# Preparing the state's coefficients two chunks ahead, instead of one, across the end of the loop

## The chip, the cores and the metric

The kernel runs on one core of one Trainium2 chip. The metric is the device time of one execution in microseconds (us). Before the change the median of three runs is 31318.25 us (31296.25 to 31333.38).

## The reference, cut to what matters

Three layers work on 8 images of 128 channels and 64 x 64 pixels: a deformable convolution (nine taps, sampled at computed offsets), a state-space scan over the 4096 pixels of each image, and a mixture of experts. The scan sets the order of everything, as each step needs the state of the step before:

```python
x_proj = x @ W_in
xs, z = jnp.split(x_proj, 2, axis=-1)
delta = xs @ W_delta
Bv = xs @ W_B
Cv = xs @ W_C
deltaA = jnp.exp(jnp.einsum('bld,dn->bldn', delta, A))
deltaB = jnp.einsum('bld,bln->bldn', delta, Bv)
def step(state, inp):
    dA_i, dB_i, x_i, C_i = inp
    state = dA_i * state + dB_i * x_i[:, None, :]
    y = jnp.einsum('bdn,bn->bd', state, C_i)
    return (state, y)
```

The state has 256 x 256 elements for each of the 8 images. `deltaA`, the coefficient of the state, is as large, and it is new at every step.

## The kernel before, in words

First `prepare` and `images` lay out the weights, normalize the images, and write the table of pixels and the records of offsets to DRAM. Then 4096 steps of the scan run for all 8 images at once. A **block** is 16 steps (`BL`), a **chunk** two steps (`CH`), so a block has 8 chunks. The loop `For_i` (L1445) makes 8 passes; the body of a pass holds 32 blocks (`BODY`), that is 512 steps and 256 chunks (`NC`), written out. Between two passes all engines meet at a barrier that belongs to L1445.

What one chunk c needs before its steps can run:

- `load_rows` (L1129): 7 DMAs on SP's queue bring the rows of delta into `rt[c % 2]`. They wait until the decays of chunk c - 2, which read that buffer, are through.
- `decays` (L1179): 19 groups of matmuls (40 in all) on PE put the products of delta and A into PSUM banks. There are three banks for this and for all other matrix work.
- `grow` (L1208): ACT takes the exponential of each group (20 instructions) into `et[c % 2]` and so frees the bank. It waits until all products of chunk c - 2, which read the same buffer, are made.
- `load_terms` (L1142): 4 DMAs on SP's queue bring the factors of the added term into `uu[c % 2]`, after the last matmul of chunk c - 2 that reads it.
- `copy_c` (L1161): ACT copies C into `zc[c % 2]`, after the contractions of chunk c - 2.

`rt`, `uu`, `zc` and `et` have two buffers each.

What one step does: the state lies in five parts. POOL multiplies the coefficients with three of them, `ht`, in SBUF (`pair`, L1305, the products `mt`, `mt`, `m`), DVE with the two others, which accumulate in PSUM (`ud` and one half of the tile `yp`; products `md` and `mh`, copied back by ACT, L1333). PE makes the added terms from `uu` (`units`, L1274), DVE adds them to `ht` (L1328), and PE contracts the products with C into y (`contract`, L1351), which is the other half of `yp`, in two operations per step.

Beside the steps runs, per block, the work of other layers: `conv_load`, `conv_gather` (nine gathers per block on POOL, L727), `conv_scale`, `conv_mix` for a block ahead; `project` (the projections of a block ahead) and `stores` (to DRAM, from where `load_rows` and `load_terms` read). `behind` (L995) is the output chain of a block that is done: it waits for y, adds the skip term (L1003), multiplies with the gate (L1008), clears y (L1011), transposes (L1016), copies to `yt` (L1023), multiplies with W_out, adds the residual (L1031), normalizes, routes, runs the experts and stores the result (L1069). In the last block of a pass the whole of `behind` lies after the last step.

The order of the instructions on each engine is set by a planner in the kernel, `Schedule` (L120), at the time the program is written. Each piece of work is a generator that yields operations with a duration; the planner keeps a clock for each engine, takes the engine that could start first, and among the operations that could start on it within a short window (200 ns on PE, 100 on ACT and DVE, 50 on POOL) the one that is due first. Due times are in steps and come from `DUE` (L71): for chunk c the decays are due from 2(c - 1) - 0.1 over 1.61 steps, the exponentials from 2(c - 1) + 0.77 over 1.65; the contractions of step j at j + 1.65 and half a step later; the operations of `behind` for block b from 16(b + 1) + 0.16 over 13.12 steps, divided by 80. A due time is a priority, no delay: what is ready and finds its engine free is done.

The chunks that are ready when the loop begins are prepared by the same generators ahead of it (L1430 to L1443). What the body then prepares is shifted against what it consumes: at the end of a pass it prepares the first chunks of the next. `before` (L1384) lists the events that the planner may take as past when a pass begins. The ranges in these three places are what the change touches.

Of the kernel before, what the change touches and what calls it, by code (L numbers as in the profile page):

```python
# [31 lines left out]
NCH = BL // CH  # L32
# [24 lines left out]
NC = SPAN // CH  # L57
# [164 lines left out]
def kernel(  # L222
# [352 lines left out]
    rt = several(2, [KR, RROW], BF, "rt")  # L575
# [550 lines left out]
    def at_chunk(c):  # L1126
        return (c // NCH) % 2, c % NCH

    def load_rows(chunks):  # L1129
        for c in chunks:  # L1130
            k, i = at_chunk(c)
            yield Due(CH * c - 3)
            yield Wait(("rows_there", c // NCH), ("decayed", c - 2))
            for n in range(GD // 2):
                yield Op(
                    SP, 400, lambda c=c, k=k, i=i, n=n: nc.sync.dma_start(  # L1136
                        out=rt[c % 2][18 * n : 18 * n + 18, RW * n : RW * n + RW],
                        in_=cells(k, RW * i + 2 * RQ * n, ((NCH * RW, 18), (1, RW))),
                    ), lat=3500, sets=[("rt", c)] * (n == GD // 2 - 1), chain=False,
                )  # L1140

    def load_terms(chunks):  # L1142
        for c in chunks:
            k, i = at_chunk(c)
            yield Due(CH * c - 1)
            yield Wait(
                ("delta_there", c // NCH), ("b_there", c // NCH), ("summed", c - 2)
            )
            for p in range(QI // 2):
                yield Op(  # L1150
                    SP, 400, lambda c=c, k=k, i=i, p=p: nc.sync.dma_start(
                        out=uu[c % 2][32 * p : 32 * p + 9].rearrange(
                            "r w b l n -> r (w b) (l n)"
                        ),
                        in_=pr[k].rearrange("i j p w b l n -> p (i j) (w b) (l n)")[
                            p, :, :, CH * DIN * i : CH * DIN * i + CH * DIN
                        ],
                    ), lat=3500, sets=[("uu", c)] * (p == 3), chain=False,
                )

    def copy_c(chunks):  # L1161
        for c in chunks:
            k, i = at_chunk(c)
            yield Due(CH * c - 0.5)
            yield Wait(("ctt", c // NCH), ("contracted", c - 2))
            yield Op(
                ACT, 110, lambda c=c, k=k, i=i: nc.scalar.copy(
                    zc[c % 2].rearrange("p s x -> p (s x)")[
                        :, 31 : 31 + 32 * NH * QI * CH
                    ].rearrange("p (s x) -> p s x", x=32)[:, :, 0].rearrange(  # L1170
                        "p (m l) -> p m l", l=CH
                    ),
                    ctt[k].rearrange("p h (b c l) -> p (h b) c l", b=QI, l=CH)[:, :, i, :],
                ), sets=[("zc", c)], chain=False,
            )
# [3 lines left out]
    def decays(chunks):  # L1179
        for c in chunks:  # L1180
            rv = rt[c % 2].rearrange("p (q g t) -> p q g t", q=GD, t=CT)
            at, span = DUE["decay"]
            yield Due(CH * (c - 1) + at, span / NG)
            yield Wait(("rt", c), *early(c))
            for g in range(NG):
                fs, n = (1, GD) if g < NG - 1 else (2, P - NA * GD)
                m = n * CT

                def decay(ps, c=c, g=g, rv=rv, fs=fs, n=n, m=m):
                    held[c, g] = ps  # L1190
                    for h in range(NH):
                        for f in range(fs):
                            mm(
                                ps[:, m * (NH * f + h) : m * (NH * f + h + 1)].rearrange(
                                    "p (q t) -> p q t", q=n
                                ),
                                alhs[:KR, g + f, P * h : P * h + P], rv[:, :n, g + f, :],
                            )

                yield Op(  # L1200
                    PE, 198 if fs == 1 else 240, decay, need="bank", chain=False,
                    sets=[("dec", c, g)] + [("decayed", c)] * (g == NG - 1),
                )
# [4 lines left out]
    def grow(chunks):  # L1208
        for c in chunks:
            yield Wait(*[  # L1210
                ("prod", CH * (c - 2) + lo, p) for lo in range(CH) for p in range(5)
            ])
            ec = et[c % 2].rearrange("p l b h d -> p h (l b) d")
            at, span = DUE["exp"]
            yield Due(CH * (c - 1) + at, span / NG)
            for g in range(NG):
                yield Wait(("dec", c, g))
                ps = held.pop((c, g))
                if g < NG - 1:
                    fs, n, d0 = 1, GD, P * (g % 2) + GD * (g // 2)  # L1220
                else:
                    fs, n, d0 = 2, P - NA * GD, NA * GD
                m = n * CT

                def exps(ec=ec, ps=ps, fs=fs, n=n, d0=d0, m=m):
                    for f in range(fs):
                        nc.scalar.activation(  # L1227
                            ec[:, :, :, P * f + d0 : P * f + d0 + n],
                            ps[:, m * f * NH : m * (f + 1) * NH].rearrange(
                                "p (h d t) -> p h t d", h=NH, d=n  # L1230
                            ),
                            AF.Exp,
                        )

                yield Op(
                    ACT, 428 if fs == 1 else 210, exps, lat=165, free=[("bank", ps)],
                    sets=[("et", c)] * (g == NG - 1), chain=False,
                )
# [145 lines left out]
    def before(n):  # L1384

        keys = []
        for b in range(n - 4, n + 1):
            keys += [(w, b) for w in (
                "rows_there", "delta_there", "b_there", "projected", "ctt", "seen",
            )]  # L1390
        for b in range(n - 6, n):
            keys += [("seen_y", b), ("out", b), ("y", b)]
        for b in range(n - 4, n + 2):
            keys += [("scaled", b), ("mixed", b), ("tnt", b)]
        for c in range(NCH * (n - 3), NCH * n + 1):
            keys += [("rt", c), ("uu", c), ("zc", c), ("et", c)]
        keys.append(("rt", NCH * n + 1))
        keys.append(("pace", n + 2))
        keys += [("pace", n + 2, i) for i in range(TAPS) if turn_of(n + 2, i) < 0]
        for c in range(NCH * (n - 3), NCH * n):  # L1400
            keys += [("decayed", c), ("summed", c), ("contracted", c)]
            keys += [("prod", CH * c + lo, p) for lo in range(CH) for p in range(5)]
        keys.append(("decayed", NCH * n))
        return keys

    def start(events):
# [23 lines left out]
    with tc.manual_schedule():  # L1430
        s = start(past)
        s.add(conv_load(range(2), lambda b: BL * b))
        s.add(conv_gather(range(2)))
        s.add(conv_scale(range(2)))
        s.add(conv_mix(range(2)))
        s.add(project(range(1)))
        s.add(stores(range(1)))
        s.add(load_rows(range(2)))
        s.add(load_terms(range(1)))
        s.add(copy_c(range(1)))  # L1440
        s.add(decays(range(1)))
        s.add(grow(range(1)))
        s.run()  # L1443

    with tc.For_i(0, NBLOCK * BL, SPAN) as i0:  # L1445
        with tc.manual_schedule():
            s = start(before(0))

            def place(b):
                return i0 + BL * b  # L1450

            s.add(behind(range(BODY), place))
            for p in (3, 4, 0, 1, 2):
                s.add(pair(p, range(SPAN)))
            s.add(units(range(SPAN)))
            s.add(contract(range(SPAN)))
            s.add(decays(range(1, NC + 1)))
            s.add(grow(range(1, NC + 1)))
            s.add(load_rows(range(2, NC + 2)))
            s.add(load_terms(range(1, NC + 1)))  # L1460
            s.add(copy_c(range(1, NC + 1)))
            s.add(stores(range(1, BODY + 1)))
            s.add(project(range(1, BODY + 1)))
            s.add(conv_load(range(2, BODY + 2), place))
            s.add(conv_gather(range(2, BODY + 2)))
            s.add(conv_scale(range(2, BODY + 2)))
            s.add(conv_mix(range(2, BODY + 2)))
            s.run()
# [43 lines left out]
```

## Time and profile before

| | |
|---|---|
| runs, median (lowest to highest) | 31318.25 us (31296.25 to 31333.38) |
| profiled execution, time | 31319.12 us |
| its span, first to last instruction | 31317.4 us |
| mean granted TensorE clock | 0.975 |
| POOL products on 128 x 1024, 8192 of them | 2369 ns each |
| POOL products on 128 x 768, 4096 of them | 1825 ns each |
| gathers (L727), 2322 of them | 975 ns each |
| exponentials (L1227), 40980 of them | 527 ns each |
| first and last pass begin (first product on POOL) | 696.46 us, 27490.84 us |

A row of the profile names line, engine, operation, the tile written and the tiles read, the shapes, the count, then the busy time in us, the mean of one in ns, and the idle time of the engine just before, with what ended it. In the timeline a row is start (us), duration (us), engine, line, operation, tiles, shapes and count, and in brackets the idle time before it and its releaser. Almost all matmuls are recorded by a helper at L690, so that the tiles tell which they are: `bank<-rt,alhs` is a decay, `up<-uu` and `ud<-uu` an added term, `yp<-mt,zc` a contraction.

### The profile page before, as it was taken

What the parts mean: (1) busy time and instruction counts of PE and PEld (TensorE: products, weight loads), DVE (VectorE), ACT (ScalarE), POOL (GpSimd) and SP (SyncE); (2) the same over time, 40 slices, a digit from 0 to 9 for tenths busy, and PEclk for the clock granted to TensorE, in tenths of its full rate; (3) what the DMA queues carried; (4) which work ended last, traced back from release to release, by engine and by line L of the source; (5) the groups of instructions that cost most, each with busy time, mean ns of one, the idle gap of its engine ahead of it and who ended that gap; (6) DMA issues with size and microseconds to landing.
All of it is one profiled execution on the core that took longest, in us unless ns stands there. A gap on an engine that the chain in (4) does not pass through costs nothing. (4 is left out here: it accounts for less than half of the span.)

```text
span 31317.4 us, 832803 instructions
## 1 busy us (share of the span) xinstructions
PE 28316.2 (90%) x304277; PEld 15352.6 (49%) x304277; DVE 26365.3 (84%) x47787; ACT 25477.9 (81%) x57905; POOL 28804.5 (92%) x14692
## 2 busy tenths in 40 slices
PE   6999989999899998999989999899998999989998
PEld 3444544454444444444444444444544444444544
DVE  5888888888888888888888888888888888888888
ACT  2888888888888888888878888888888888878888
POOL 1999999999999999999999999999999999999999
PEclk7999999999999999999999999999999999999999
DMA  7222222222222222222222222222222222222222
GB/s 165 59 58 59 59 56 59 58 60 57 58 57 60 58 59 56 60 59 58 60 55 59 57 60 58 57 58 59 59 57 58 57 60 58 59 56 60 59 57 56
DMA packets 4785814, 1907.20 MB, mean 61 GB/s; under 512 B 3445459, under 2 KB 4595944, under 8 KB 4780656
## 3 DMA queue, kind: packets, MB, share of 16 engines
q1 hardware_dynamic: 4578504, 1187.48, 19.6%
q0 software_dynamic: 195232, 639.15, 7.5%
q8 instruction: 2421, 39.67, 0.6%
q10 hardware_dynamic: 7944, 26.87, 0.3%
q14 instruction: 1713, 14.03, 0.2%
HBM read 1284.96 MB, written 566.60 MB: 59 GB/s over the span
## 5 line engine op out<-in xcount | busy, mean ns | idle before, releaser
L1227 ACT ACTIVATE et<-bank 128x448 f32<-128x448 f32 (+1 forms) x40980 | 19046.1, 527 | 3611.4 <-PE bank L690 2990.6
L1313 POOL TENSOR_TENSOR mt<-et,ht 128x1024 f32<-128x1024 f32 x8192 | 19277.1, 2369 | 1450.0 <-PE yp L690 859.0
L690 PE MATMUL bank<-rt,alhs 126*128 126x224 bf16 (+1 forms) x81960 | 12265.7, 254 | 1450.1 <-ACT et L1227 648.7
L1328 DVE TENSOR_TENSOR ht<-mt,up 128x1024 f32<-128x1024 f32 x8192 | 9969.5, 1217 | 2637.0 <-PE ud L690 1846.6
L690 PEld LDWEIGHTS <-alhs 126*128 126x128 bf16 x81960 | 6761.8, 98 | 7657.1 <-issue 6817.9
L690 PE MATMUL yp<-mt,zc 128*32 128x256 f32 x65536 | 8711.5, 388 | 154.5 <-ACT yp L1333 57.0
L1313 POOL TENSOR_TENSOR m<-et,ht 128x768 f32<-128x768 f32 x4096 | 7476.9, 1825 | 38.2 <-DVE ht L1328 10.9
L690 PE MATMUL up<-uu 32*128 32x256 bf16 x45056 | 4832.3, 275 | 600.7 <-DVE ht L1328 521.6
L1313 DVE TENSOR_TENSOR md<-et,ud 128x1024 f32<-128x1024 f32 x4096 | 4975.0, 1215 | 113.3 <-PEq L1445 43.4
L690 PE MATMUL yp<-m,zc 128*32 128x256 f32 x24576 | 4449.4, 391 | 151.3 <-POOL m L1313 143.1
L1328 DVE TENSOR_TENSOR ht<-m,up 128x768 f32<-128x768 f32 x4096 | 3893.4, 951 | 566.3 <-PE up L690 524.6
L1333 ACT COPY ud<-md 128x1024 f32<-128x1024 f32 x4096 | 4275.3, 1044 | 97.4 <-DVE md L1313 84.9
L690 PE MATMUL yp<-md,zc 128*32 128x256 f32 x32768 | 4353.8, 387 | 0.0
L690 PEld LDWEIGHTS yp<-mt,zc 128*32 128x32 f32 x65536 | 3271.6, 109 | 1620.2 <-issue 533.9
L690 PEld LDWEIGHTS <-uu 32*128 32x128 bf16 x65541 | 1616.1, 92 | 3121.3 <-issue 2878.9
L727 POOL DMA_INDIRECT g<-table,rec x2322 | 2264.1, 975 | 413.9 <-issue 254.1
L690 PE MATMUL yp<-mh,zc 128*32 128x256 f32 x8192 | 2480.0, 385 | 0.0
L1313 DVE TENSOR_TENSOR mh<-et,yp 128x256 f32<-128x256 f32 x4096 | 1706.5, 417 | 446.0 <-PE yp L690 423.4
L690 PEld LDWEIGHTS yp<-m,zc 128*32 128x32 f32 x24576 | 1587.7, 109 | 921.5 <-issue 421.2
L1333 ACT COPY yp<-mh 128x256 f32<-128x256 f32 x4096 | 1596.2, 390 | 346.6 <-PE yp L690 207.4
L760 DVE SCALAR_TENSOR_TENSOR bank<-g,rec,bank 128x128 f32<-128x128 f32 x4644 | 1641.6, 353 | 84.6
L690 PE MATMUL ud<-uu 32*128 32x256 bf16 x16388 | 1621.5, 276 | 0.0
(207 smaller groups left out, 22799.8 us busy)
## 6 DMA issues: line engine op xcount, KB each, us to landing
rt<-rz SPq DMA_DIRECT2D x14350, 22.5 KB
uu<-pr SPq DMA_DIRECT2D x8196, 36.0 KB
pr<-dpt SPq DMA_DIRECT2D x3084, 48.0 KB
pr<-bpt SPq DMA_DIRECT2D x3084, 48.0 KB
rz<-dst SPq DMA_DIRECT2D x6939, 21.0 KB
table<-xc SPq DMA_DIRECT2D x24, 1690.0 KB
g<-table,rec POOLq DMA_INDIRECT x2322, 3.5
rec<-recs SPq DMA_DIRECT2D x2064, 2.8 KB
```

Source lines behind the costliest of these rows:

```text
L690: nc.tensor.matmul(out, lhs, rhs, start=start, stop=stop, **kw)
L727: nc.gpsimd.indirect_dma_start(out=g, out_offset=None, in_=table, in_offset=bass.IndirectOffsetOnAxis(ap=rec[b % 2].bitcast(I32)[:, j : j ...
L760: nc.vector.scalar_tensor_tensor(out, gq, s, acc, ALU.mult, ALU.add)
L1227: nc.scalar.activation(ec[:, :, :, P * f + d0 : P * f + d0 + n], ps[:, m * f * NH : m * (f + 1) * NH].rearrange("p (h d t) -> p h t d", h= ...
L1313: (nc.gpsimd if g < QP else nc.vector).tensor_tensor(like(g, m), part(g, c, lo), like(g, state[g]), ALU.mult)
L1328: lambda m=m: nc.vector.tensor_tensor(ht[g], m, up[:, :n], ALU.add),
L1333: ACT, act_ns(n, True), lambda m=m: nc.scalar.copy(state[g], m),
```

## The change

Everything that belongs to chunk 1 of a pass moves across the end of the loop: ahead of the loop the loads, decays, exponentials and the copy of C are made for chunks 0 and 1 instead of chunk 0 (and the rows of delta loaded for three chunks instead of two); the body prepares chunks 2 to 257 instead of 1 to 256 (rows: 3 to 258 instead of 2 to 257), and the events taken as past are extended accordingly. Buffers, due times and the operations themselves stay as they are. The pass thus ends with the decays and exponentials of chunk 257, which is chunk 1 of the next pass.

```diff
@@ -1392,15 +1392,15 @@
-        for c in range(NCH * (n - 3), NCH * n + 1):
+        for c in range(NCH * (n - 3), NCH * n + 2):
             keys += [("rt", c), ("uu", c), ("zc", c), ("et", c)]
-        keys.append(("rt", NCH * n + 1))
+        keys.append(("rt", NCH * n + 2))
...
-        keys.append(("decayed", NCH * n))
+        keys += [("decayed", NCH * n + c) for c in range(2)]
@@ -1435,11 +1435,11 @@
-        s.add(load_rows(range(2)))
-        s.add(load_terms(range(1)))
-        s.add(copy_c(range(1)))
-        s.add(decays(range(1)))
-        s.add(grow(range(1)))
+        s.add(load_rows(range(3)))
+        s.add(load_terms(range(2)))
+        s.add(copy_c(range(2)))
+        s.add(decays(range(2)))
+        s.add(grow(range(2)))
@@ -1454,11 +1454,11 @@
-            s.add(decays(range(1, NC + 1)))
-            s.add(grow(range(1, NC + 1)))
-            s.add(load_rows(range(2, NC + 2)))
-            s.add(load_terms(range(1, NC + 1)))
-            s.add(copy_c(range(1, NC + 1)))
+            s.add(decays(range(2, NC + 2)))
+            s.add(grow(range(2, NC + 2)))
+            s.add(load_rows(range(3, NC + 3)))
+            s.add(load_terms(range(2, NC + 2)))
+            s.add(copy_c(range(2, NC + 2)))
```

## The prediction, made before the change was run

> **What bounds the kernel now.** I read the page's busy shares first, then the waits, then the timeline around the loop's ends, because the change touches nothing else.
>
> ```profile
> span 31317.4 us, 832803 instructions
> PE 28316.2 (90%) x304277; PEld 15352.6 (49%) x304277; DVE 26365.3 (84%) x47787; ACT 25477.9 (81%) x57905; POOL 28804.5 (92%) x14692
> L1227 ACT ACTIVATE et<-bank 128x448 f32<-128x448 f32 (+1 forms) x40980 | 19046.1, 527 | 3611.4 <-PE bank L690 2990.6
> ```
>
> POOL is the busiest: per step it makes three products, 2 x 2.369 + 1.825 = 6.56 us, and 0.55 us of gathers (2264.1 / 4096), against a step of 7.42 us. A chunk of two steps needs 20 exponentials on ACT, 9.3 us (19046.1 / 2049), in about 14.8 us. The view of waits has the loop's end in one row:
>
> ```profile
> POOL mt L1313 <- POOLq L1445: 186.3, 7, 27.0
> ```
>
> Seven times POOL stands still for 26.6 us. The timeline around the last of these ends (27464 to 27491) shows why:
>
> ```profile
> 27462.58 1.84 POOL L1313 TENSOR_TENSOR m<-et,ht 128x768 f32<-128x768 f32 x1
> ...
> 27467.32 0.49 DVE L1003 SCALAR_TENSOR_TENSOR yp<-dlt,qt,yp 128x256 f32<-128x256 f32 x1 [0.62 <-PE yp L690]
> ...
> 27470.02 0.71 PE L690 MATMUL bank<-wout_sb,yt 128*128 128x128 f32 x4 [0.46 <-ACT yt L1023]
> ...
> 27486.61 0.41 SPq L1069 DMA_DIRECT2D out<-ot  x1
> ...
> 27490.84 4.68 POOL L1313 TENSOR_TENSOR mt<-et,ht 128x1024 f32<-128x1024 f32 x2 [26.42 <-POOLq L1445]
> ```
>
> After the last product of step 511 (27464.42) the block's output chain (`behind`) runs alone: y complete, L1003 at +2.9 us, product with W_out at +5.6, norm, router, experts, store at +22.2, landing and the loop's barrier to +26.4. ACT is busy 2.79 us of these 26. So there is room in which to compute something; the question is whether that takes anything off the path, and whether it pushes this chain.
>
> **What is taken from the loop's head.** Before, chunk 1's decays (PE) and exponentials (ACT) run beside steps 0 and 1:
>
> ```profile
> 27491.82 2.29 ACT L1227 ACTIVATE et<-bank 128x448 f32<-128x448 f32 x5 [0.75 <-PE bank L690]
> 27493.96 1.07 ACT L1333 COPY ud<-md 128x1024 f32<-128x1024 f32 x1
> ...
> 27497.48 2.38 POOL L1313 TENSOR_TENSOR mt<-et,ht 128x1024 f32<-128x1024 f32 x1 [0.19 <-DMA rt<-rz]
> ...
> 27502.30 0.78 ACT L1227 ACTIVATE et<-bank 128x448 f32<-128x448 f32 x3 [0.17 <-PE bank L690]
> ...
> 27510.06 4.66 POOL L1313 TENSOR_TENSOR mt<-et,ht 128x1024 f32<-128x1024 f32 x2
> 27510.14 1.42 ACT L1227 ACTIVATE et<-bank 128x448 f32<-128x448 f32 x3 [3.19 <-POOL m L1313]
> ```
>
> Chunk 1 is complete at 27503.08 and POOL first reads it at 27510.06, without a wait: 7.0 us of slack. POOL's time there goes into its products and five gathers in a row (27500.01 to 27505.98, L727), which are due at once whatever `et` holds. Chunk 2 cannot start earlier either: there are two `et` buffers, and its exponentials wait for step 1's last product (27510.11). From there all is as before: the lead cannot grow beyond one chunk. So the head gives back only what ACT's exponentials cost step 0: the copy of `ud` (27493.96) stands behind 5 + 2 of them, and the second step starts later than 6.42 us after the first by 1.17, 0.07, 1.12, 0.33, 1.11, 1.36 and 0.22 us in the seven later passes: **-5.4 us** in all. Bounds: 0 (another wait takes its place) and, with the issue gaps between gathers (4 x 0.30), -14.
>
> **What is put at the loop's end.** Chunk 257's decays: 19 groups, 40 matmuls; 20 exponentials, 9.3 us of ACT; a copy of C (0.25 us); on SP 7 loads of `rt` and 4 of `uu`. None can come before the products of step 511 end, since they overwrite the buffer that step 511 reads. So all of it falls beside the output chain, from 27464.7 to about 27475. SP's 11 loads take about 2.4 + 1.4 us of its queue (27496.41 and 27499.09 show 2.64 and 1.41) and wait for the last unit (27467.2); they are issued by about 27472, 14 us before the store at 27486.61, so I cost them at nothing; without that cover 3.8 us per end.
>
> On PE and ACT the order is fixed by due times. Decays of chunk 257 have 511.9 to 513.4, exponentials 512.8 to 514.3; step 511's two contractions 512.65 and 513.15; the chain's operations 512.16 growing by 0.164 each: transposes 512.8, copy of `yt` 513.1, product with W_out 513.5, everything from the norm on beyond 514.4. Hence three effects. (1) Decays that find a bank go ahead of the contractions that complete y. Every ordinary block shows the price:
>
> ```profile
> 27346.13 1.83 POOL L1313 TENSOR_TENSOR m<-et,ht 128x768 f32<-128x768 f32 x1
> ...
> 27353.86 0.48 DVE L1003 SCALAR_TENSOR_TENSOR yp<-dlt,qt,yp 128x256 f32<-128x256 f32 x1
> ```
>
> There L1003 starts 5.9 us after the block's last product, with 16 decay matmuls in between, against 2.9 at the loop's end: 3.0 us later. (2) From y on, VectorE is free, so L1003, L1008, transposes and the copy of `yt` take the 2.3 us they take now, to +8.2, plus at most one exponential (0.5). (3) The product with W_out needs a bank, and the remaining decays are due before it. They are handed out as exponentials end: 20 in 9.3 us from +0.3; the last of 19 decays takes the bank that the 16th exponential group frees, at 0.3 + 16 x 0.49 = +8.1, and the product the next one, once `yt` is copied (8.2 + 0.5 + 0.4): at about +9.3 instead of +5.6. Later steps find ACT and the banks free. **+3.7 us per end**, 8 x 3.7 = **+29.6 us** (the last pass does it too, for nothing). Bounds: 0 (the chain is never pushed) and 9.4 (it stands until the whole 9.3 us is done, with 0.1 for the release): 0 to +75.
>
> **The entry.** No barrier stands before the first pass. Chunk 0's exponentials end at 696.4 and POOL starts at 696.46. With chunk 1's queued directly behind (9.3 us, to about 705.8), step 0's `ud` copy moves from 699.18 to 705.8, `ud` accumulates and `ht` is added (0.4 + 1.2) by about 708.7, and the second step starts there, not at 702.88: **+5.8 us**, once; between 0 and 10. SP's three added issues there (rt, uu: 3.8 us) put the gathers' records at about 710, when POOL wants them at 711.
>
> **Between.** From the third to the thirty-first block of a pass the order of instructions on DVE (184 per block) and ACT (225) is the same, block after block. The schedule falls into one cycle within two blocks, so I expect the same cycle after the change and count 0 for those 29 blocks.
>
> The sum: 31319.1 (the profiled execution; span 31317.4) - 5.4 + 29.6 + 5.8 = 31349. The median shown, 31318.25, is 0.9 below that execution, so I leave it: **31349 us, 0.10% slower**, inside the 0.2% that I take as what this kernel's measurement can tell from no change.
>
> **A rule on the clock.** The granted clock is 1.00 to 27469, 0.69 from 27469 to 27474, 0.50 from 27474 to 27490, and 0.52 in the first 5 us of the pass. In the head the first `ht` would be ready at 27495.6 (from 27490.87, by 1.22 + 1.05 + 0.4 + 1.22 and handovers) and is wanted at 27497.3, 1.7 us later, so slow matmuls cost nothing there in my sum.
>
> The Trainium skill, "TensorE: Matmul & The Clock Gate", Part 1, says that the array falls to half rate after about 3.4 us of idleness and comes back after about 3.4 us of work, which these rows fit. It speaks for the tail (decays would keep PE warm to +10, and the 1.12 us of matmuls of 27469 to 27474 would lose some 0.4 us: 31346 instead of 31349) and against the head, where 40 fewer matmuls warm it (up to 8 us more if every pass lost 1 us by it).
>
> **Rivals.**
> - *Hidden altogether* (0.15): contractions go first and the chain threads between exponentials. 0 at the ends, -5.4 at the heads, +5.8 at the entry: 31319. For: ACT idles 23 of 26 us. Against: the due times, and +5.9 in ordinary blocks.
> - *Slower, the chain starved* (0.13): the output chain does not get past chunk 257 and waits for all of its exponentials. 8 x 9.4 + 5.8 - 5.4 = +75.6: 31395. It decides from about 7.8 us per end, (62.6 - 0.4) / 8. For: every decay is due before the W_out product. Against: transposes and the `yt` copy are due first.
> - *Another cycle* (0.10): the new start of the pass leads the order of work into another cycle. Blocks now take 117.0 to 122.4 us; 1.4 us off the mean of 118.8 over 29 x 8 blocks is 325 us either way: about 31025 or 31675, counted from the forecast. Half each.
> - *It does what it says, at a gain*: freed engines in block 0 save the waits of 1.5 us (27537) and 3.2 us (27607): 8 x 4.7 = -38 with the ends at +29.6 and the entry gives 31317; it is part of the first.
>
> **How the numbers follow.** The forecast has 0.62: 31325 to 31380. The range takes in the first rival and the starved chain: 31310 to 31400; left out is the other cycle (0.10) and some 0.05 of tails. Slower by over 0.2% (above 31381): starved 0.13, half of the other cycle 0.05, tail of the forecast 0.02 = 0.20. Faster: 0.05. Within: 0.75.
>
> **What would show it.** POOL's standstill at line 1445 grows from 26.6 to about 30 us; L1003 comes about 5.9 us after the last product there and the W_out product about 9; 20 exponentials lie between. The second step starts 6.4 us after the first in every pass, POOL reads chunk 1 without waiting, and the head is otherwise unchanged. Blocks 3 to 31 keep their 184 and 225 instructions in the same order; if not, my largest assumption is wrong. If L1003 stays at +2.9, the due times do not act as I read them.

## The result, and the profile after

| | before | after |
|---|---|---|
| median of 16 runs each, on the same chip | 31325.62 us (31284.91 to 31339.15) | 31401.24 us (31371.41 to 31432.55) |
| ratio of the medians | | 1.0026 [1.0019, 1.0033] |
| profiled execution | 31319.12 us | 31373.26 us |
| its span | 31317.4 us | 31371.5 us |
| mean granted clock | 0.975 | 0.975 |

The change makes the kernel 0.26% slower. The forecast was 31349 us, +30; the medians differ by +75.6 and the two profiled executions by +54.1 (the profiled execution of after is among the shortest of its 16 runs). The page of after, its head and two rows, shows nothing of it in the shares:

```profile
span 31371.5 us, 832806 instructions
PE 28338.2 (90%) x304317; PEld 15341.5 (49%) x304317; DVE 26363.5 (84%) x47787; ACT 25482.9 (81%) x57926; POOL 28813.7 (92%) x14692
L1227 ACT ACTIVATE et<-bank 128x448 f32<-128x448 f32 (+1 forms) x41000 | 19043.0, 527 | 3569.0 <-PE bank L690 2902.8
```

20 exponentials more (41000 against 40980), 40 matmuls more, the same busy times to 0.1%. The time came from waits. The view of waits has the first half of it:

```profile
POOL mt L1313 <- POOLq L1445: 222.2, 7, 31.8
```

Seven times 31.74 us (31.64 to 31.82) from the last product of a pass to the first of the next, instead of 26.61; the eighth end, behind the last pass, went from 32.79 to 37.61. Together +40.8 us where the prediction had +29.6.

The timeline around the last of these ends, in the order of time (the last product ends at 27511.62):

```profile
27516.56 0.49 DVE L1003 SCALAR_TENSOR_TENSOR yp<-dlt,qt,yp 128x256 f32<-128x256 f32 x1 [0.69 <-PE yp L690]
27516.82 5.15 ACT L1227 ACTIVATE et<-bank 128x448 f32<-128x448 f32 x13
27517.08 0.42 DVE L1008 TENSOR_TENSOR yy<-yp,szt 128x256 f32<-128x256 f32 x1
27517.42 3.75 PE L690 MATMUL bank<-rt,alhs 126*128 126x224 bf16 x20 [0.25 <-ACT et L1227]
27521.35 0.33 PE L822 MATMUL bank<-ident,tn 128*128 128x128 f32 x1 [0.19 <-ACT et L1227]
27521.79 0.44 PE L1016 MATMUL bank<-ident,yy 128*128 128x128 f32 x2
27522.69 0.71 PE L690 MATMUL bank<-wout_sb,yt 128*128 128x128 f32 x4 [0.46 <-ACT yt L1023]
...
27539.28 0.41 SPq L1069 DMA_DIRECT2D out<-ot  x1
```

L1003 starts at +4.94, where the prediction said 5.9; `yy` is ready at 27517.50. Then PE runs 20 decay matmuls, half of the chunk, before L1016 transposes `yy` at +10.17, 4.3 us after it could have. The product with W_out comes at +11.07 instead of +5.60, and the store at +27.66 instead of +22.19. From the product on, nothing more is lost.

The second half lies where nothing was changed. The blocks of a pass, by the times between POOL's first products (mean of passes 2 to 8, profiled executions): block 0 124.0 before and 123.2 after, block 1 **116.7 and 123.9**, block 2 118.2 and 117.0, block 3 118.5 and 117.3. Over all eight passes these four blocks took 3822.1 and 3858.2 us: +36.1 (block 1 alone +57.1). The view of windows, for blocks 0 and 1 of the last pass, first of before, then of after (us, busy time and count of PE, PEld, DVE, ACT, POOL, the clock, the DMA share, GB/s):

```profile
27490.84:27616.48 125.64, 107.79 (x1134) 58.95 (x1136) 94.28 (x147) 96.44 (x217) 116.76 (x63) 0.93 0.29 66
27616.48:27733.13 116.65, 106.82 (x1179) 57.48 (x1177) 101.23 (x186) 98.52 (x225) 112.36 (x58) 1.00 0.27 59
```

```profile
27543.33:27666.70 123.37, 105.63 (x1102) 54.84 (x1102) 95.80 (x150) 87.61 (x197) 116.85 (x62) 0.92 0.28 65
27666.70:27790.28 123.58, 109.01 (x1174) 59.27 (x1176) 99.87 (x183) 98.79 (x226) 112.56 (x58) 0.99 0.25 57
```

In block 0, ACT has lost 8.8 us of work (20 exponentials) and POOL idles 6.5 us instead of 8.9. In block 1 POOL has the same work (112.6 against 112.4) and idles 11.0 us instead of 4.3.

The rest has two parts. The first pass begins at 690.84 us instead of 696.46 (-5.6), but 4.8 of this was there before anything that the change touches: the copy L906 ahead of the loop starts at 655.33 instead of 660.14. From that copy to the second chunk of the first pass (716.50 after, 716.59 before) it is 61.2 us instead of 56.5, because the second step starts 12.90 us after the first instead of 6.42. So the entry costs 4.7 us, and this execution hides it by an early start. Blocks 4 to 31 are 17 us shorter in sum (0.08 us each) with the same instructions. -5.6 + 40.8 + 36.1 - 17 gives the +54.1. A second profile of the changed kernel, on another chip (third group below), has neither the early start (697.97 us, and again 61.3 us from L906 to the second chunk) nor the short blocks (26586.7 us for blocks 4 to 31, against 26562.6 here and 26579.8 before). Without these two it is about +76, near the medians' +75.6.

The head's own term went as predicted. POOL and ACT of the last pass:

```profile
27543.33 4.69 POOL L1313 TENSOR_TENSOR mt<-et,ht 128x1024 f32<-128x1024 f32 x2 [31.71 <-POOLq L1445]
27547.97 1.84 POOL L1313 TENSOR_TENSOR m<-et,ht 128x768 f32<-128x768 f32 x1
27549.74 2.37 POOL L1313 TENSOR_TENSOR mt<-et,ht 128x1024 f32<-128x1024 f32 x1
27552.24 0.98 POOL L727 DMA_INDIRECT g<-table,rec  x1
```

```profile
27544.67 0.37 ACT L906 COPY xst<-bank 128x256 f32<-128x256 f32 x1 [5.43 <-PE bank L690]
...
27562.41 3.16 ACT L1227 ACTIVATE et<-bank 128x448 f32<-128x448 f32 x7 [0.76 <-POOL m L1313]
```

The second step starts 6.41 us after the first (6.40 to 6.43 in all later passes), chunk 1 is read without a wait, and chunk 2's exponentials cannot start before +19.1, behind the last product that reads their buffer. But the first row of ACT is new: L906, a copy in `project` of block 1, runs 1.3 us into the pass; before it ran at +12.1:

```profile
27502.95 0.39 ACT L906 COPY xst<-bank 128x256 f32<-128x256 f32 x1
```

### The profile page after: what moved, and what is told of

Same layout as the page of the kernel before. It is cut to its first block, busy times and chain, and to the rows that moved or that the text cites. A ratio compares the mean times of both kernels' runs of the same rounds, so it can differ in the third digit from the quotient of the medians.

```text
span 31371.5 us, 832806 instructions
## 1 busy us (share of the span) xinstructions
PE 28338.2 (90%) x304317; PEld 15341.5 (49%) x304317; DVE 26363.5 (84%) x47787; ACT 25482.9 (81%) x57926; POOL 28813.7 (92%) x14692
## 5 line engine op out<-in xcount | busy, mean ns | idle before, releaser
L1313 POOL TENSOR_TENSOR m<-et,ht 128x768 f32<-128x768 f32 x4096 | 7480.1, 1826 | 40.8 <-DVE ht L1328 13.0
```

The source lines that it names most:

```text
L1313: (nc.gpsimd if g < QP else nc.vector).tensor_tensor(like(g, m), part(g, c, lo), like(g, state[g]), ALU.mult)
```

## The experiments

Two causes were to be tried. **Theory A**: the ends cost what they cost because decays of chunk 257, due before the transposes, hold PE, the banks and the planner's token. **Theory B**: block 1 is slow because `project(1)`, released from behind chunk 1's exponentials, starts 10.8 us earlier and shifts the side work into another order. The rivals: the loads on SP, the extra work as such, or a third cost that neither names.

### First group: each cause taken away by itself

*Decays and exponentials of chunk 257 due after the output chain:*

```diff
 decays, grow:
-            yield Due(CH * (c - 1) + at, span / NG)
+            yield Due(CH * (c - 1) + at + (30 if c > NC else 0), span / NG)
```

> The changed kernel, with the due times of chunk 257's decays and exponentials 30 steps later, so that the output chain of the last block goes ahead of them wherever both could start. Theory A (the end of the pass): POOL's standstill at the loop's end grew from 26.6 to 31.7 us only because of the order, since the transposes of the output chain stand behind all decays; in the right order the chunk fits into the chain's gaps. Then the standstill falls to 26.6 to 28.5 us, and the time by 25 to 41 us against the changed kernel, to 1.0013 to 1.0018 of the kernel before; block 1 of each pass stays at 123.5 us. Rival A' (the work itself: 9.3 us of ACT and the three banks are needed by the chain whatever the order): standstill 30.5 to 32, 1.0024 to 1.0028.

*`project(1)` not before step 0 is through:*

```diff
-            yield Wait(("tnt", b))
+            yield Wait(("tnt", b), *([("prod", 0, 2)] if b == 1 else []))
```

> The changed kernel, but project for block 1 also waits for the third product of step 0, so that it can't start at once on the engines that chunk 1's work no longer holds. Theory B (block 1): the second block of each pass takes 123.8 instead of 116.7 us because project for block 1 starts some 12 us earlier than before and leads the side work of the first two blocks into another order. Then block 1 returns to 116.5 to 118.5 us, the standstill stays at 31.7, and the time falls by 25 to 55 us to 1.0009 to 1.0018 of the kernel before. Rival B' (the later gathers or chunk 2's exponentials do it, whenever project starts): block 1 stays at 122 to 125, 1.0024 to 1.0028.

*Both:*

> Both edits together. If A and B hold and nothing else costs, the time is that of the kernel before within 20 us, 0.9993 to 1.0007, with a standstill of 26.6 to 28.5 and block 1 at 116.5 to 118.5. If both rivals hold, 1.0024 to 1.0028. If it stays above 1.0010 with both places back at their old values, a third cost is hidden in the first block or the entry.

*The body without chunk 257's decays and exponentials* (the state of chunk 1 of passes 2 to 8 is then made with stale coefficients):

```diff
-            s.add(decays(range(2, NC + 2)))
-            s.add(grow(range(2, NC + 2)))
+            s.add(decays(range(2, NC + 1)))
+            s.add(grow(range(2, NC + 1)))
```

> The changed kernel without chunk 257's decays and exponentials: chunk 1 of each later pass uses the coefficients left over in the buffer, so this part of the computation is left out, to measure its whole price at the end of the pass. Theory A and its rival agree here: standstill 26.4 to 27.0 us, 8 x 5.1 = 41 us less than the changed kernel, 1.0011 to 1.0016 of the kernel before, and block 1 at 123 to 125. If the time falls by less than 25 us, the end of the pass isn't where the time went.

| (before: 31321.71 us) | median, us | ratio | standstill, us | block 1, us |
|---|---|---|---|---|
| chunk 257 due late | 31344.01 | 1.0007 [0.9998, 1.0016] | 27.63 | 124.2 |
| project(1) later | 31378.46 | 1.0016 [1.0007, 1.0025] | 31.90 | 117.6 |
| both | 31332.36 | 1.0003 [0.9994, 1.0012] | 27.54 | 118.3 |
| chunk 257 left out | 31348.39 | 1.0006 [0.9997, 1.0015] | 26.55 | 123.5 |

(Standstill and block 1 are means over the later passes of the profiled execution.) Each edit removes its own half and leaves the other where it was. Two of the totals came out below what was expected, chunk 257 due late (1.0013 to 1.0018) and chunk 257 left out (1.0011 to 1.0016), though within what their intervals allow; the places came out as expected. The timeline of PE with chunk 257 due late (the last product ends at 27472.58):

```profile
27475.67 0.33 PE L822 MATMUL bank<-ident,tn 128*128 128x128 f32 x1
...
27476.88 0.79 PE L690 MATMUL bank<-rt,alhs 126*128 126x224 bf16 x4 [0.18 <-ACT et L1227]
27477.76 0.44 PE L1016 MATMUL bank<-ident,yy 128*128 128x128 f32 x2
27478.19 0.79 PE L690 MATMUL bank<-rt,alhs 126*128 126x224 bf16 x4
27478.89 0.71 PE L690 MATMUL bank<-wout_sb,yt 128*128 128x128 f32 x4
27479.44 2.65 PE L690 MATMUL bank<-rt,alhs 126*128 126x224 bf16 x14
```

The same decays now run around the chain: transposes at +5.2, the product with W_out at +6.3. What stays is 1.0 us per end. With both edits there is no difference left that the measurement can tell; its interval leaves room for a third cost of up to 0.12%, some 38 us, not for one of the size of either half. Leaving the work out altogether gives the standstill of before and still the slow block 1: the two halves are separate. And 26.55 without the work, 27.63 with it in this order, 31.74 as changed: of the 5.1 us per end about 1 is the work, the rest its order.

### Second group: the loads, the token, the gathers

On another chip, where the kernel before takes 31586.7 us.

*The loads, the rows and C two chunks ahead, the decays and exponentials as before:*

```diff
 against the changed kernel:
-            s.add(decays(range(2, NC + 2)))
-            s.add(grow(range(2, NC + 2)))
+            s.add(decays(range(1, NC + 1)))
+            s.add(grow(range(1, NC + 1)))
```

> One part of the change alone: the loads of rt and uu and the copy of C run one chunk further ahead across the loop's end, decays and exponentials stay as in the kernel before. All theories: the loads have 14 us of cover at the end and nothing waits for them at the head, so standstill 26.4 to 27.0, block 1 at 116.5 to 117.5, time 0.9994 to 1.0006 of the kernel before. Over 1.0012: SP's queue does cost something, and the part given to decays and exponentials is too large.

31588.29 us, 1.0000 [0.9991, 1.0009]; standstill 26.32, block 1 117.5. The 11 loads on SP cost nothing that can be told, as predicted; the loss comes from decays and exponentials.

*The transposition L822 of `conv_mix` at once.* Why do the transposes of `yy`, due before most decays, run behind them? Work that needs a bank takes one token first, `stage`, of which there is one (`take`, L693; its holder gives it back with the bank, L641). In the timeline of after, L822 comes just ahead of L1016: `conv_mix` could have had the token and waited for a bank behind decays due before it, while the transposes waited for the token. If that is so, an early L822 frees the transposes:

```diff
             yield Wait(("seen", b - 1))
+            if b in (2, BODY + 1):
+                yield Due(0.0)
             wk = yield from take(lambda wk: nc.tensor.transpose(wk[:, :P], tn, ident), P)
```

> The changed kernel, with the last transposition of conv_mix (L822) for blocks 2 and 33 due at once. Theory C: both losses have one mechanism, the single token 'stage' of the planner. The transposition takes the token, then waits for a bank behind all decays that are due before it, and the output chain, although due earlier, waits for the token (block 1: normalized at 120.2, transposed only at 143.2, the chain's yt at 145.8 us of the pass; end of the pass: transposed after the last decay). Then block 1 returns to 117 to 119.5 us, at the end the chain's transposes no longer stand behind all decays, and the standstill falls from 31.7 to 29.5 to 31 (the W_out product is still due after the decays). Time 1.0005 to 1.0017 of the kernel before. Rival C' (the token isn't it; project's early start crowds the block by its own work): block 1 stays at 122 to 125, the standstill at 31.5 or more, 1.0022 to 1.0028.

31653.38 us, 1.0020 [1.0011, 1.0029]: the total was missed. PE at the last end (L1018 is the old L1016), with POOL's last product, which ends at 27757.79, and the old L1003:

```profile
27755.42 2.37 POOL L1315 TENSOR_TENSOR mt<-et,ht 128x1024 f32<-128x1024 f32 x1 [0.54 <-PE yp L690]
...
27759.21 0.49 DVE L1005 SCALAR_TENSOR_TENSOR yp<-dlt,qt,yp 128x256 f32<-128x256 f32 x1 [0.17 <-PE yp L690]
...
27760.40 2.10 PE L690 MATMUL bank<-rt,alhs 126*128 126x224 bf16 x10 [0.25 <-ACT et L1229]
27762.59 0.33 PE L1018 MATMUL bank<-ident,yy 128*128 128x128 f32 x1
...
27763.21 0.27 PE L1018 MATMUL bank<-ident,yy 128*128 128x128 f32 x1
...
27764.01 2.29 PE L690 MATMUL bank<-rt,alhs 126*128 126x224 bf16 x14 [0.19 <-ACT et L1229]
27766.48 0.71 PE L690 MATMUL bank<-wout_sb,yt 128*128 128x128 f32 x4 [0.19 <-ACT et L1229]
```

Now the transposes start at +4.8 and stand before the last decays, as the prediction had it, and the product with W_out comes at +8.7, once the decays are through. The standstill fell to 29.33. But it is counted from POOL's last product, and that came late: step 511 takes 9.6 us from its first product to the end of its last, 6.5 in before and after, and the old L1003 starts at +1.4. From there to the product with W_out it is 7.3 us, against 6.1 in after. The last block is longer, too, 120.8 us, where in the other kernels it takes 116 to 118; with the standstill it makes 150.1 us, against 148.4 in after (about 1 us of this is the chip's, whose ordinary blocks are longer). So at the end of the pass the early L822 brought the transposes forward and won nothing, and what part of the 5.1 us is the token's this run does not show. Block 1 took 119.9, as Theory C has it but for 0.4 us.

*The first five gathers of block 2 brought behind the last product of a pass*, on the kernel before: in the head they stand between POOL's products (27552.24 above), so they could be what keeps block 0 long. (In this kernel and the next, the gathers at the entry overwrite buffers from which the last taps of block 1 are still to be read; the convolution of block 1, pixels 16 to 31, is changed by it.)

```diff
             for j in pick(b):
+                if b == BODY + 2:
+                    yield Wait(("prod", SPAN - 1, 2))
...
-            s.add(conv_gather(range(2, BODY + 2)))
+            s.add(conv_gather(range(2, BODY + 3), pick))
```

> The kernel before, without the change, but with the first five gathers of the block that is due at the head of the next pass issued behind the last product of a pass, where POOL stands still, and their records loaded earlier. Theory D: what holds up the head is POOL's five gathers in a row (6.3 us), not the exponentials. Then block 0 falls from 124.0 to 117.5 to 119.5 us, the standstill stays at 26.4 to 27.2, and the time falls by 35 to 50 us, 0.9983 to 0.9990. With the gathers gone, chunk 1's exponentials (done 11.7 to 13.4 us after the start) come close to where POOL wants them (12.9), so a wait of up to 1 us for ACT may show there. If the standstill grows by what block 0 loses, nothing is won: 0.9997 to 1.0005.

*The same with the change and chunk 257 due late:*

> The gathers moved as in e8, together with the change and late due times for chunk 257's decays and exponentials. If the gathers were the cover that made the change worthless at the head, the change is now worth 0.5 to 2 us per head (no wait for chunk 1, second step at 6.4 us), against 1.0 us that the standstill grows (27.6 instead of 26.6): the same as e8 within 15 us, 0.9981 to 0.9990. If block 1 takes 123 or more again, it is 0.9996 to 1.0004.

31594.69 us, 1.0003 [0.9994, 1.0012], and 31578.42 us, 0.9996 [0.9987, 1.0005]. Block 0 fell to 121.1 and 119.2 us (128.6 with the loads alone on this chip), but the standstill grew to 31.66 and 32.27. The timeline of the first of them, POOL, then DVE, around the last product (it ends at 27673.89; L1016 is the old L1003):

```profile
27674.03 0.98 POOL L734 DMA_INDIRECT g<-table,rec  x1
...
27679.08 0.95 POOL L734 DMA_INDIRECT g<-table,rec  x1 [0.30 <-issue]
```

```profile
27676.14 1.22 DVE L1341 TENSOR_TENSOR ht<-mt,up 128x1024 f32<-128x1024 f32 x1 [1.73 <-PE up L690]
27681.41 0.49 DVE L1016 SCALAR_TENSOR_TENSOR yp<-dlt,qt,yp 128x256 f32<-128x256 f32 x1 [4.04 <-remote]
```

The last gather ends at +6.1. Until +7.5 ACT stands for 7.29 us and DVE for all but one addition (27676.14), and L1003 comes at +7.5 instead of +2.9. So in these two kernels the gathers cost at the start of the output chain what they save in the head; the first was expected at 0.9983 to 0.9990 or, if the standstill took back what block 0 loses, at 0.9997 to 1.0005, and it is the latter; the second, expected at 0.9981 to 0.9990, isn't below before either. Between the two, block 0 is 1.9 us shorter with the change, and block 1 1.7 us (117.8 against 119.5). That this comes from the decays and exponentials taken from the head is not shown; the second step with the change, expected at 6.4 us, starts at 8.5.

### Third group: the changed kernel again, and three ends of these threads

(before: 31338.21 us)

*The changed kernel once more:*

> The changed kernel once more, as the measure for the others of this batch, since the chips differ by up to 0.9%. All theories: 1.0019 to 1.0033 of the kernel before, standstill 31 to 32 us, block 1 6 to 8 us longer than the mean of the later blocks would have it in the kernel before.

31430.51 us, 1.0027 [1.0017, 1.0038]; standstill 31.79, block 1 124.1: the same as in the first result.

*L822 at once in block 2 alone:* as above, with `if b == 2`.

> The changed kernel with the last transposition of conv_mix due at once for block 2 alone, nothing else, so that the end of the pass stays as it is. Theory C (the token 'stage' is held by that transposition, and the output chain of block 0 waits for it): block 1 falls by 4 to 7 us per pass against the changed kernel on the same chip and the standstill stays at 31 to 32; time 1.0008 to 1.0018 of the kernel before, if blocks 2 and 3 don't give it back. Rival C' (crowding by project itself): block 1 within 1.5 us of the changed kernel's, 1.0019 to 1.0033.

31401.13 us, 1.0018 [1.0009, 1.0027]; block 1 119.4 instead of 124.1, standstill 32.55, 0.8 above that of the changed kernel. So most of block 1's loss, 4.7 of some 7 us, goes with L822. The view of one line shows how, first after, then this kernel (L824 is the old L822; the last pass begins at 27543.33 and at 27565.78):

```profile
L822 PE MATMUL bank<-ident,tn x1: 328/328/328, 27686.6 to 27686.6; 128*128 128x128 f32 x1
```

```profile
L824 PE MATMUL bank<-ident,tn x1: 332/332/332, 27685.9 to 27685.9; 128*128 128x128 f32 x1
```

+143.3 and +120.1. And the copy of `yt` behind it, for before, after and this kernel (passes begin at 27490.84, 27543.33 and 27565.78):

```profile
L1023 ACT COPY yt<-bank x1: 479/479/479, 27624.5 to 27624.5; 128x256 f32<-128x256 f32 x1
```

```profile
L1023 ACT COPY yt<-bank x1: 427/427/427, 27689.2 to 27689.2; 128x256 f32<-128x256 f32 x1
```

```profile
L1025 ACT COPY yt<-bank x1: 367/367/367, 27702.3 to 27702.3; 128x256 f32<-128x256 f32 x1
```

+133.7, +145.9, +136.5. In before, `tn` of `conv_mix(2)` is written at +132.8, when the transposes of block 0 have begun (+132.3), and L822 follows at +153. In after it is written at +120.3, *before* block 0's y is complete (L1003 at +125.1), so `conv_mix(2)` can take the token first. It then waits for a bank for 23 us behind decays that are due earlier: from +109.2 to +142.9 the matmuls on the banks are 94 decays in a row. (In before L822 waits 20 us, too, but with the transposes ahead of it.) The output chain of block 0 is 12 us late by then, and its work and that of the next block fall together in block 1.

How the early `project(1)` leads there is open. With `project(1)` held back (first group; its last pass begins at 27533.58) block 1 took 117.6, and yet `tn` is written as early as in after, at +119.3, and L822 still comes ahead of the transposes. But it comes at +134:

```profile
L822 PE MATMUL bank<-ident,tn x1: 332/332/332, 27667.6 to 27667.6; 128*128 128x128 f32 x1
```

`yt` is then copied at +135.9. So it is not the early `tn` alone, but how long L822 waits for its bank. Why that is 23 us in one order and 15 in the other, and why 119.4 is not 116.7, was not taken apart further.

*Gathers behind the last product, but held back until the residual sum is made, at the entry behind the last taps of block 1; with the change and chunk 257 due late:*

```diff
-                    yield Wait(("prod", SPAN - 1, 2))
+                    hold = j == 0
+                    yield Wait(("prod", SPAN - 1, 2), ("out", BODY - 1))
+                    if hold:
+                        yield Op(POOL, 100, lambda: nc.gpsimd.tensor_copy(pz, t2[:, :1]))
```

> As e9, with the five gathers at the end of the pass held back until the residual sum of the last block's output chain (a copy of one column on POOL waits for it), so that they don't run while y is finished. Theory E (in e8 and e9 the gathers themselves held up whatever ran beside them between 3 and 8 us after the last product): the standstill falls from 32.3 to between 27 and 30 us, block 0 stays at 6 to 9 us under that of the kernel before, and the time is 0.9980 to 0.9992. Rival E' (whenever they run in the chain, they cost it 4 to 5 us): standstill 31 or more, 0.9992 to 1.0002.

*The same, held back until the gate is made* (`gate[:, :1]` in place of `t2[:, :1]`):

> As e11, but held back until the router's gate, about 14 us behind the last product in the kernel before, so that they run beside the experts' products and the store. Theory E: standstill 27 to 30, 0.9980 to 0.9992. Rival E': 31 or more, 0.9992 to 1.0002. Between the two kernels the lower standstill tells which part of the chain bears the gathers.

The first: 31341.81 us, 0.9998 [0.9989, 1.0007]; standstill 27.46, block 0 119.6, block 1 118.0. The stall of the gathers is gone (they run from +8.5 to +14.5 beside small operations), block 0 is 4.3 us shorter than in before (6 to 9 had been expected), and yet the total is not below before by what can be told; a gain had been expected. (These places are those of its shortest execution, 31299.13 us, the one that was profiled.) The second: 31397.12 us, 1.0017 [1.0008, 1.0026], above what either theory had; standstill 32.51, where 27 to 30 had been expected, or 31 and more by the rival. POOL at its last end:

```profile
27556.95 0.95 POOL L738 DMA_INDIRECT g<-table,rec  x1 [0.30 <-issue]
27565.25 2.35 POOL L1331 TENSOR_TENSOR mt<-et,ht 128x1024 f32<-128x1024 f32 x1 [7.35 <-POOLq L1464]
```

Its store is issued at 27556.08, +23.3 as in the first (27456.50, +23.5), but the pass begins at +32.5 instead of +27.7. Between lies POOL's part of the barrier, the instruction DRAIN, here in before and then in this kernel (start in us, duration in ns):

```profile
L1445 POOLq DRAIN  x1: 8111/8111/8111, 27462.6 to 27462.6; - x1
```

```profile
L1464 POOLq DRAIN  x1: 10218/10218/10218, 27554.0 to 27554.0; - x1
```

It ends 6.3 us after POOL's last instruction, in before at 27470.7 after a product that ends at 27464.42, here at 27564.2 after a gather that ends at 27557.90; in the first of the pair, at 27453.75, it is 6.3 us again. So the wait is not one for gathers: in these kernels POOL's last work, of either kind, must be done 6.3 us before POOL's part of the barrier is. In before the output chain covers this; here it stands at the end of the pass. The rival's number came true, not its reason. The standstills with blocks 0 to 3 account for some 25 of the 59 us that this kernel is slower; the rest lies in blocks 4 to 31, 63.6 us longer than in before in the profiled execution. Their order is as before, but more of them run at a lower clock (last section); why is open.

No version is below the kernel before by more than the measurement can tell.

## Why the prediction was wrong in size, point by point

The sign of the sum was right, its size was not: +30 in the forecast, +54.1 in the profiled execution, +75.6 in the medians. The time lies just past the upper end of the range. Two steps failed, and the larger is that the head was taken as "otherwise unchanged" and "Between" counted at 0: block 1, which no term prices, took +57 us in the eight passes. The other is effect (2) of the end, +11. That the rival "the chain starved" has +75.6 as well is chance: it needs 9.4 us per end, or at least 7.8 to decide, and measured are 5.1; the rest comes from blocks that it doesn't mention.

- **Head, -5.4 us: right as a term.** The second step starts at 6.41 us in every later pass, and block 0 of these passes is 5.5 us shorter in sum. What failed is "the head is otherwise unchanged": see "Between".
- **Loads at no cost: right** as far as the loads alone can tell (1.0000 [0.9991, 1.0009]).
- **Effect (1) of the end, right and a little too high**: L1003 at +4.9, not +5.9.
- **Effect (2) of the end: failed.** "L1003, L1008, transposes and the copy of `yt` take the 2.3 us they take now … plus at most one exponential". From L1003 (+4.94) to the copy of `yt` they took 5.7 us. The decays were through at +9.5 (27521.17), about where effect (3) has the bank for the W_out product (+9.3); but the transposes, which were to be done long before, came only then, and the product at +11.07. The step looked only at the due times of transposes and decays, of which the transposes have the earlier. By the planner's code and by the order of the rows, L822 just ahead of L1016, the token stood between them, held by an operation due later than both: priorities don't order work behind a lock that a low priority holds. The end cost 5.1 us instead of 3.7 (+40.8 in all instead of +29.6). That the 1.4 us are the token's was not isolated: the run with an early L822 won nothing at the end.
- **Hidden altogether**, the first rival, wanted contractions first; that is what late due times give: L1003 at +2.9, and 1.0 us per end is left of 5.1. So the cost of the end was one of order, not of the 9.3 us of work.
- **The entry, +5.8 us: right, a little too high.** The second step of the first pass starts 6.5 us later than before, counted from the first, and the entry costs 4.7 us; that the profile of after shows none of it is due to an early start in work that was not changed.
- **"Between", 0 us: right in the cycle, wrong in the count.** From the fourth block on DVE's 184 and ACT's 225 instructions stand in the order of before, so "another cycle" did not come. But the forecast priced blocks 3 to 31 and said nothing of the two blocks in which the order settles. Block 1 took some 7 us more in each of eight passes; blocks 2 and 3 took 21 us less in sum, most of it by fewer stretches of low clock (last section), so that the first four blocks make 36.1 us net. The rows of the head had shown `project(1)` waiting behind the exponentials that the change takes away; what moved up behind them was not followed.
- **The clock.** Granted in before and after, 5 us each from a pass's start (before from 27490.8, after from 27543.3):

```profile
27490.80:27495.80 5.00, 4.55 (x39) 2.54 (x40) 1.55 (x2) 4.22 (x9) 4.96 (x3) 0.60 0.04 4
27495.80:27500.80 5.00, 4.46 (x54) 2.30 (x50) 4.38 (x5) 4.79 (x11) 4.67 (x3) 1.00 0.37 68
```

```profile
27543.30:27548.30 5.00, 4.42 (x30) 3.02 (x34) 2.44 (x3) 1.59 (x3) 4.97 (x3) 0.50 0.04 7
27548.30:27553.30 5.00, 3.37 (x28) 1.20 (x22) 4.15 (x6) 2.00 (x4) 4.79 (x3) 0.50 0.28 47
27553.30:27558.30 5.00, 5.00 (x45) 1.77 (x37) 2.86 (x5) 0.62 (x1) 3.84 (x5) 0.59 0.85 184
```

The clock stays at half rate some 10 us longer, yet the second step is in time: the first `ht` is ready at 27548.63 and POOL takes it at 27549.74, so that 1.1 us of the slack that the sum counted are left. The Trainium skill, "TensorE: Matmul & The Clock Gate", Part 1, says that the clock follows how busy PE has lately been. The rows agree in the number of matmuls, 58 in these ten microseconds instead of 93, and less clearly in PE's busy time, 4.42 us of the first five against 4.55. The 0.4 us per end that the prediction worked out from the page for the tail does not show: from the W_out product to the store it is 16.59 us before and after.

## What to carry to other kernels

Where a planner hands out one lock, look for who holds it when an urgent operation wants it: an operation with a late due time that takes the lock first holds up everything behind it until its own turn comes; here 94 matmuls with earlier due times went ahead of it. Work taken from a place that has slack frees what queued behind it; follow that work until the order repeats, and price each block on the way. And work put into an idle stretch costs by its order, not its length: the 9.3 us of exponentials cost 5.1 us per end in one order and 1.0 in another.

## What the runs showed of the hardware that was not expected

- Five indirect gathers on POOL, 0.95 us each with 0.30 us between them, next to the end of the step: ACT and, but for one addition, DVE did nothing until 1.4 us after the last of them (+7.5 us). What held them, the trace names only "remote". Held back by 8 us, the same gathers delayed none of it.
- POOL's DRAIN at the loop's barrier ended 6.3 us after POOL's last instruction, after a product as after a gather.
- Blocks with the same order of instructions take four lengths: in before, blocks 4 to 30 of all passes take about 117.0 us (64 of them), 118.3 (66), 119.9 (74) or 122.5 (12), and the granted clock over the block goes with it: 1.00, 0.99, 0.97 and 0.94 (the third figure from the right in the rows below). By the trace's records of the clock these are blocks with none, one, two and four stretches of 3.41 us at half rate. The changed kernel has the same four lengths, 65, 68, 70 and 13 times. So the spread of 117.0 to 122.4 us on which the prediction built "another cycle" is the clock's and not the order's. Gathers held back until the gate: 59, 59, 77 and 21.

```profile
29036.87:29156.83 119.96, 110.11 (x1183) 60.11 (x1178) 101.72 (x185) 98.91 (x226) 112.26 (x59) 0.97 0.27 58
29156.83:29275.07 118.24, 108.50 (x1183) 58.36 (x1178) 101.60 (x185) 98.99 (x226) 112.43 (x58) 0.99 0.27 58
29391.99:29508.96 116.97, 107.26 (x1183) 58.08 (x1178) 101.51 (x185) 98.88 (x226) 112.27 (x58) 1.00 0.27 60
29508.96:29631.61 122.65, 112.82 (x1183) 60.80 (x1178) 101.57 (x185) 99.47 (x226) 112.33 (x59) 0.94 0.26 56
```

- Two chips gave 31321.71 and 31586.7 us for the kernel before, 0.85% apart: only ratios on one chip compare. In the profiles a block without a half-rate stretch takes 117.0 us in before and 118.3 in the kernel with the loads alone, which ran on the slower chip, so the granted clock doesn't make this difference.
